# A two-bit search, a turned gate and smaller first pieces in the prologue of an expert-choice FFN

## The chip, the cores and the metric

The kernel runs on one core of a Trainium2 chip. The time is the device time of one execution in microseconds (us): the median of three runs is 4277.47 us (4274.08 to 4278.06). One more execution was profiled; the lines of the profile that this text shows come from it. In them PE is the tensor engine, PEld its weight loads, DVE the vector engine, ACT the scalar engine, POOL the GpSimd engine and SP the engine that issues most DMAs.

## The reference, cut to what matters

Six layers run over 4096 tokens of 256 features: an expert-choice FFN, an attention, the same FFN again, a routed FFN, another attention, the routed FFN again. The change touches only the expert-choice FFN, which occurs twice, on the layer-normalized rows:

```python
S = jax.nn.sigmoid(xt @ Wg).T            # 8 experts x 4096 tokens
G, I = jax.lax.top_k(S, k)               # k = 1024: each expert chooses its tokens
ex = xt[I]
hid = gelu(einsum('ekh,ehf->ekf', ex, W1) + b1)
out = (einsum('ekf,efh->ekh', hid, W2) + b2) * G[..., None]
new_x = zeros_like(xt).at[I].add(out)
x = x + 0.5 * new_x
```

## The kernel before, in words

The rows lie in SBUF as 32 tiles of 128 tokens. `_ffn0` computes one expert-choice FFN, and on PE, DVE, ACT and POOL the order of its instructions is the order of the program text. It has a prologue, which ends in the list of rows of the first expert, and then a loop over eight experts that gathers rows, multiplies and scatter-adds. `tile_kernel` calls it twice, first with `n` 0, at the start of the program, and then with `n` 1, after the first attention.

The prologue's front works in eight groups of four tiles (`QT` is 4). `ln_range` takes mean and variance of eight tiles on DVE (L151, L152), and makes `rstd` from them with one square root on ACT (L160). `rows(g)` normalizes the group's four tiles, two on DVE and two on POOL (L234), into one of three buffers `xn`, and stores them to `xn_d` in DRAM. `columns(g)` turns them on PE, in eight transposes (L244), and ACT copies the result to `xnT` (L245). `logits(g)` multiplies with the gate (L250): the 128 tokens of a tile are stationary, and the gate's 8 columns move, in two halves of the features, so that each of the group's four tiles takes two matmuls of 128x128 stationary and 8 moving columns. All logits lie in one PSUM tile `lg`. In the loop over the groups `logits` runs one group behind `columns`. `sigmoid(0, 24)` and `sigmoid(24, TT)` make the scores on DVE and ACT (L262 to L266); the first stands ahead of the last group's logits.

The search follows. The scores are turned so that each of the 128 partitions holds 256 of the scores of one expert, 16 partitions to an expert. The 1024th largest score of each expert is found bit by bit, on the scores' own bits: `search` runs over the upper 15 bits and then over the lower 15 (`M` is 15), so there are 30 rounds. In one round ACT scales the values (`v`, L315, ahead of time, in four buffers), DVE counts the values that are at least the threshold `at` (L317, with an accumulator), PE adds the counts of an expert's 16 partitions by a matmul with the 0/1 matrix `same` (L307, into `cnt`), and DVE makes the next threshold from the count (L321, L325):

```python
nc.vector.tensor_scalar(junk, v, at[:, 0:1], None, ALU.is_ge, ALU.add, accum_out=r)
total(cnt, self.same, r)
nc.vector.tensor_scalar(nxt, at, 2.0, -0.5, ALU.mult, ALU.add)
nc.vector.scalar_tensor_tensor(at, cnt, float(K0), nxt, ALU.is_ge, ALU.add)
```

In the first round `lower_bits` makes the lower half of the values on DVE behind the count. Then ties are settled, each chosen token gets its place in its expert's list (L344 to L380), and `indices` (L388 to L410) writes the list with one-hot matmuls. POOL gathers the rows by it (L419). PE's first matmul of the experts is L448.

Of the kernel before, what the change touches and what calls it, by code (L numbers as in the profile page):

```python
# [9 lines left out]
F32 = mybir.dt.float32  # L10
BF16 = mybir.dt.bfloat16
I32 = mybir.dt.int32
AF = mybir.ActivationFunctionType
ALU = mybir.AluOpType
# [6 lines left out]
P = 128  # L21
B, S, D = 8, 512, 256
NT = B * S
TT = NT // P
DC = D // P
QT = S // P
# [3 lines left out]
E0, FF = 8, 1024  # L30
K0 = NT * 2 // E0
# [11 lines left out]
E1, INTER, SHARED = 16, 128, 256  # L43
N_GROUPS, TOPK_GROUPS, TOPK = 4, 2, 4


FULL = TT * TOPK
SLOTS = FULL + E1

CH = 512  # L50
# [9 lines left out]
class Kernel:  # L60
    def __init__(self, ctx, tc, w):
        self.tc, self.nc, self.w = tc, tc.nc, w
        nc = self.nc
        self.const = const = ctx.enter_context(tc.tile_pool(name="const", bufs=1))
        resid = ctx.enter_context(tc.tile_pool(name="resid", bufs=1))
        self.dram = ctx.enter_context(tc.tile_pool(name="dram", bufs=1, space=DRAM))


        self.late = self.wide = None


        self.x = resid.tile([P, TT, D], F32, name="x")
        x_in = w["x"].rearrange("(t p) d -> p t d", p=P)
        for g in range(TT // QT):
            ts = slice(g * QT, g * QT + QT)
            nc.sync.dma_start(out=self.x[:, ts, :], in_=x_in[:, ts, :])

        self.ident = const.tile([P, P], F32, name="ident")
        make_identity(nc, self.ident)
        self.ones = const.tile([P, P], F32, name="ones")  # L80
        nc.gpsimd.memset(self.ones, 1.0)

        self.tri = const.tile([P, P], F32, name="tri")
        nc.gpsimd.affine_select(
            out=self.tri, in_=self.ones, compare_op=ALU.is_gt, fill=0.0,
            base=0, pattern=[[1, P]], channel_multiplier=-1,
        )

        iota_i = const.tile([P, P], I32, name="iota_i")
        nc.gpsimd.iota(iota_i, pattern=[[1, P]], base=0, channel_multiplier=0)  # L90
        self.iota = const.tile([P, P], F32, name="iota")
        nc.vector.tensor_copy(self.iota, iota_i)

        lane_i = const.tile([P, 1], I32, name="lane_i")
        nc.gpsimd.iota(lane_i, pattern=[[1, 1]], base=0, channel_multiplier=1)
        self.lanes = const.tile([P, 1], F32, name="lanes")
        nc.vector.tensor_copy(self.lanes, lane_i)
        self.bands = const.tile([P, 2, TT // 2], F32, name="bands")
        nc.vector.tensor_copy(self.bands, iota_i[:, 0:TT].rearrange("p (j c) -> p c j", c=2))

        self.iota_h = const.tile([P, P], BF16, name="iota_h")
        nc.vector.tensor_copy(self.iota_h, iota_i)

        self.same = const.tile([P, P], F32, name="same")
        runs = self.same.rearrange("p (e j) -> p e j", j=P // E0)
        ones = self.ones.rearrange("p (e j) -> p e j", j=P // E0)
        nc.gpsimd.affine_select(
            out=runs, in_=ones, compare_op=ALU.is_ge, fill=0.0,
            base=0, pattern=[[-(P // E0), E0], [0, P // E0]], channel_multiplier=1,
        )  # L110
        nc.gpsimd.affine_select(
            out=runs, in_=runs, compare_op=ALU.is_ge, fill=0.0,
            base=P // E0 - 1, pattern=[[P // E0, E0], [0, P // E0]], channel_multiplier=-1,
        )
        self.before = const.tile([P, P], F32, name="before")
        nc.gpsimd.tensor_tensor(self.before, self.same, self.tri, ALU.mult)

        self.desc = const.tile([P, E1], F32, name="desc")
        nc.vector.tensor_scalar(self.desc, self.iota[:, 0:E1], -1.0, float(E1), ALU.mult, ALU.add)

        self.slots_d = self.dram.tile([SLOTS * P, D], F32, name="slots_d")
        self.ys_d = self.dram.tile([SLOTS * P, D], F32, name="ys_d")
# [76 lines left out]
    def _ffn0(self, ctx, n, beside):  # L199
        nc, tc, w = self.nc, self.tc, self.w  # L200
        pool = ctx.enter_context(tc.tile_pool(name=f"f0_{n}", bufs=1))
        work = ctx.enter_context(tc.tile_pool(name=f"f0w_{n}", bufs=2))
        psum = ctx.enter_context(tc.tile_pool(name=f"f0p_{n}", bufs=2, space=PSUM))
# [9 lines left out]
        wg = pool.tile([P, DC, E0], F32, name="wg")  # L213
# [12 lines left out]
        lg = psum.tile([P, TT, E0], F32, name="lg", tag="rt", bufs=1)  # L226
        stats = mv, rstd = self.ln_tiles(pool)
        xns, xnTs = {}, {}

        def rows(g):  # L230
            xn = xns[g] = work.tile([P, QT, D], F32, name="xn", bufs=3)
            for i in range(QT):
                t = g * QT + i
                (nc.vector, nc.gpsimd)[i % 2].tensor_scalar(  # L234
                    xn[:, i, :], self.x[:, t, :], mv[:, t, 0:1], rstd[:, t : t + 1], ALU.subtract, ALU.mult
                )
            nc.sync.dma_start(out=xn_rows[:, g * QT : g * QT + QT, 0:D], in_=xn)

        def columns(g):
            xnT = xnTs[g] = work.tile([P, DC, CH], F32, name="xnT", bufs=2)  # L240
            for c in range(DC):
                tp = psum.tile([P, CH], F32, name="tp", tag="tp")
                for i in range(QT):
                    nc.tensor.transpose(tp[:, i * P : i * P + P], xns[g][:, i, c * P : c * P + P], self.ident)  # L244
                nc.scalar.copy(xnT[:, c, :], tp)  # L245

        def logits(g):
            for i in range(QT):
                for c in range(DC):
                    nc.tensor.matmul(  # L250
                        lg[:, g * QT + i, :], lhsT=xnTs[g][:, c, i * P : i * P + P], rhs=wg[:, c, :],
                        start=(c == 0), stop=(c == DC - 1),
                    )

        raw = pool.tile([P, TT, E0], F32, name="raw")

# [2 lines left out]
        def sigmoid(t0, t1):  # L259
            r = raw[:, t0:t1, :]  # L260

            nc.vector.tensor_scalar(r, lg[:, t0:t1, :], -87.0, None, ALU.max)  # L262
            nc.scalar.activation(r, r, AF.Exp, scale=-1.0)
            nc.vector.tensor_scalar(r, r, 1.0, None, ALU.add)
            nc.vector.reciprocal(r, r)
            nc.vector.tensor_copy(s[:, :, :, t0 // 2 : t1 // 2], r.rearrange("p (j c) e -> p c e j", c=2))  # L266

        self.ln_range(pool, stats, 0, 8)
        for g in range(TT // QT):
            if g % 2 == 0 and g < 6:  # L270
                self.ln_range(pool, stats, (g // 2 + 1) * 8, 8)
            rows(g)
            columns(g)
            if g > 0:
                logits(g - 1)
        wts = weights(0)
        sigmoid(0, 24)
        logits(TT // QT - 1)
        sigmoid(24, TT)
        nc.sync.dma_start(out=xn_rows[:, :, D:], in_=raw)  # L280
        for g in range(4):
# [8 lines left out]

        M = 15
        sp = psum.tile([P, 2, P], F32, name="sp", tag="tp")
        for c in range(2):
            nc.tensor.transpose(sp[:, c, :], s[:, c].rearrange("p e j -> p (e j)"), self.ident)
# [3 lines left out]
        high = pool.tile([P, D], F32, name="high")  # L300
        nc.vector.tensor_copy(high, high_i)
        low_i = pool.tile([P, D], I32, name="low_i")
        low = pool.tile([P, D], F32, name="low")
        junk = pool.tile([P, D], F32, name="junk")

        def total(out, weights, r):
            nc.tensor.matmul(out, lhsT=weights, rhs=r, start=True, stop=True)  # L307

        def search(vals, between):

            at = work.tile([P, 1], F32, name="at", bufs=4)
            nc.vector.memset(at, 0.5)
            for b in range(M - 1, -1, -1):
                v = work.tile([P, D], F32, name="v", bufs=4)
                nc.scalar.mul(v, vals, 0.5 ** (b + 1))  # L315
                r = work.tile([P, 1], F32, name="r", bufs=2)
                nc.vector.tensor_scalar(junk, v, at[:, 0:1], None, ALU.is_ge, ALU.add, accum_out=r)  # L317
                cnt = psum.tile([P, 1], F32, name="cnt", tag="psI", bufs=1)
                total(cnt, self.same, r)
                nxt = work.tile([P, 1], F32, name="nxt", bufs=2)  # L320
                nc.vector.tensor_scalar(nxt, at, 2.0, -0.5, ALU.mult, ALU.add)  # L321
                if b == M - 1:
                    between()
                at = work.tile([P, 1], F32, name="at", bufs=4)
                nc.vector.scalar_tensor_tensor(at, cnt, float(K0), nxt, ALU.is_ge, ALU.add)  # L325
            return at

        def lower_bits():
            nc.vector.tensor_scalar(low_i, bits, (1 << M) - 1, None, ALU.bitwise_and)
            nc.vector.tensor_copy(low, low_i)  # L330

        at = search(high, lower_bits)

        vals = pool.tile([P, D], F32, name="vals")
        nc.vector.tensor_scalar(vals, high, at[:, 0:1], 0.5, ALU.subtract, ALU.add)
        nc.vector.scalar_tensor_tensor(vals, vals, float(1 << M), low, ALU.mult, ALU.add)
        at = search(vals, lambda: None)


        one_row = pool.tile([P, D], F32, name="one_row")  # L340
# [1677 lines left out]
```

## Time and profile before

| what | us |
|---|---|
| median of three runs | 4277.47 |
| the profiled execution | 4273.81 |
| its span, first to last instruction | 4271.7 |
| PE busy | 3817.9 (89%) |
| DVE busy | 1929.9 (45%) |
| ACT busy | 1461.2 (34%) |
| POOL busy | 1229.9 (29%) |
| first prologue: first statistics, first transposes, last logits read by DVE, first count, last count's result, first gather | 4.9, 17.1, 58.5, 62.2, 107.0, 121.7 |
| second prologue: the same | 1468.9, 1482.3, 1523.8, 1527.5, 1572.0, 1586.7 |

The page's second part cuts the span into 40 slices of 106.8 us and gives the busy tenths of each engine; PEclk is the granted share of the tensor engine's clock in tenths. The granted clock over the whole span is 0.904. A busy share is an average over stages with different limits, so that what the change is worth is read from the timeline and the waits of the two prologues.

### The profile page before, as it was taken

The numbers are of one execution on the slowest core, as the hardware profiler recorded it, in microseconds if no ns is written. First come the engines' busy times: TensorE is split into PE (matmuls) and PEld (weight loads), VectorE is DVE, ScalarE is ACT, GpSimd is POOL, SyncE is SP. The second block draws the span as 40 slices with busy tenths as digits, with TensorE's granted clock in tenths as the row PEclk, the third lists the DMA queues.
The fourth block names the chain that finished last, engine by engine and source line by source line (L and its number), as shares of the span: only waits on it lengthen the run. The fifth ranks groups of instructions, "written<-read, shape, count | busy, mean of one in ns | idle before, by whom it ended". The sixth has DMA issues, their size and how long they took to land.

```text
span 4271.7 us, 51994 instructions
## 1 busy us (share of the span) xinstructions
PE 3817.9 (89%) x17660; PEld 2304.8 (54%) x17660; DVE 1929.9 (45%) x5057; ACT 1461.2 (34%) x3371; POOL 1229.9 (29%) x1132
## 2 busy tenths in 40 slices
PE   5789896999999759889878998999999999998998
PEld 5456663333333446566546784545545555457774
DVE  4321204555554441121166366665555546555455
ACT  2122222333343212222223343444444443443441
POOL 2233224223231113223136251221000011461256
PEclk6899997889996559999979999999999999998999
DMA  5223225700000212223334470100000000115664
GB/s 186 50 65 66 56 39 185 244 17 17 23 11 21 73 40 53 69 61 67 65 119 165 153 248 22 30 27 9 1 1 1 1 1 1 40 56 160 195 198 130
DMA packets 262995, 316.67 MB, mean 74 GB/s; under 512 B 31696, under 2 KB 232784, under 8 KB 262480
## 3 DMA queue, kind: packets, MB, share of 16 engines
q1 hardware_dynamic: 213584, 212.12, 15.9%
q0 software_dynamic: 49152, 101.24, 9.7%
q8 instruction: 146, 2.39, 0.2%
q14 instruction: 113, 0.93, 0.1%
HBM read 157.81 MB, written 147.06 MB: 71 GB/s over the span
## 4 chain that ended last, share of the span: by engine, by line
PE 60%; DVE 9%; ACT 5%; issue 5%; DMA 3%; POOL 0%; POOLq 0%; DVEq 0%; ACTq 0%; SPq 0%
PE pq L997 5%; PE hs L1664 5%; PE op L459 5%; PE sp L1023 5%; PE zp L1057 5%; PE hp L448 5%; PE tp L1044 4%; PE st L769 3%; PE pv L978 3%; PE yp L1087 3%; PE yps L1684 2%; PE hp L1580 2%; PE pp L637 2%; ACT ex L1032 2%; DMA yg<-ys_d,slot 2%
## 5 line engine op out<-in xcount | busy, mean ns | idle before, releaser
L1032 ACT ACTIVATE ex<-sp,nmax 128x512 f32<-128x512 f32 x512 | 347.4, 689 | 411.1 <-DVE nmax L1029 388.9
L459 PE MATMUL op<-w,hid 128*128 128x256 f32 x2048 | 473.2, 394 | 0.0
L448 PE MATMUL hp<-exT,w 128*128 128x512 f32 x1024 | 448.0, 596 | 0.0
L459 PEld LDWEIGHTS op<-w,hid 128*128 128x128 f32 x2048 | 406.8, 199 | 66.1 <-issue 8.6
L466 POOL DMA_INDIRECT acc_d<-ob,idx x128 | 199.7, 1560 | 689.1 <-ACT ob L465 387.2
L1432 POOL DMA_INDIRECT yg<-ys_d,slot x256 | 266.5, 1041 | 411.2 <-DVE x L1451 194.4
L464 DVE TENSOR_TENSOR ob<-op,b 128x256 f32<-128x256 f32 x128 | 54.4, 425 | 663.8 <-PE op L459 640.3
L1029 DVE TENSOR_REDUCE nmax<-sp 128x2 f32<-128x1024 f32 x256 | 303.2, 1218 | 72.3 <-PE sp L1023 72.1
L1044 PEld LDWEIGHTS tp<-ident,ex 128*128 128x128 f32 x2048 | 226.9, 141 | 190.6 <-issue 129.3
L1664 PE MATMUL hs<-w_sb,xT 128*128 (+1 forms) x1152 | 312.1, 395 | 19.1 <-DVE as L1672 11.3
L448 PEld LDWEIGHTS hp<-exT,w 128*128 128x128 f32 x1024 | 195.2, 192 | 232.0 <-issue 231.2
L740 DVE CUSTOM_DVE_ANT_0 junk<-sp,mask 128x128 f32<-128x128 f32 (+3 forms) x512 | 248.5, 485 | 133.0 <-PE sp L733 113.4
L1044 PE MATMUL tp<-ident,ex 128*128 128x128 f32 x2048 | 275.4, 278 | 36.2 <-ACT eT L187 35.8
L452 ACT ACTIVATE hid<-hp,b 128x512 f32<-128x512 f32 x256 | 175.9, 687 | 338.4 <-PE hp L448 338.4
L1023 PE MATMUL sp<-qk,qk 64*128 64x512 f32 x1024 | 261.7, 630 | 1.9 <-ACT ex L1032 1.9
L997 PE MATMUL pq<-xnT,wide 128*128 128x512 f32 x512 | 252.0, 616 | 5.6 <-DVE eT L189 4.7
L778 ACT ACTIVATE ex<-st 128x1024 f32<-128x1024 f32 (+3 forms) x256 | 173.9, 703 | 240.5 <-DVE st L776 240.4
L1064 POOL COPY wide<-rec 128x512 f32<-128x512 f32 x64 | 39.2, 612 | 714.8 <-PE rp L1070 605.2
L1250 POOL DMA_INDIRECT slots_d<-wide,slot x176 | 175.0, 994 | 233.4 <-DVE lane L1387 102.2
L465 ACT ACTIVATE ob<-ob,gate 128x256 f32<-128x256 f32 x128 | 65.0, 508 | 510.7 <-DVE ob L464 510.7
L1057 PE MATMUL zp<-eT,v 128*64 128x512 f32 x1024 | 235.2, 600 | 0.0
L1664 PEld LDWEIGHTS hs<-w_sb,xT 128*128 128x128 f32 x1152 | 202.9, 196 | 46.1 <-issue 10.8
(325 smaller groups left out, 6092.2 us busy)
## 6 DMA issues: line engine op xcount, KB each, us to landing
xs<-slots_d SPq DMA_DIRECT2D x70, 512.0 KB, 5.4
ys_d<-ys SPq DMA_DIRECT2D x70, 512.0 KB, 3.5
w<-in_W SPq DMA_DIRECT2D x32, 1024.0 KB, 5.6
slots_d<-mask SPq DMA_DIRECT2D x8, 2304.0 KB, 10.9
ys_d<-mask SPq DMA_DIRECT2D x8, 2304.0 KB, 17.9
w_sb<-in_w SPq DMA_DIRECT2D x24, 512.0 KB, 7.6
xn_d<-xn SPq DMA_DIRECT2D x16, 512.0 KB, 4.3
acc_d<-x SPq DMA_DIRECT2D x8, 1024.0 KB, 5.1
```

The lines of the kernel that those rows point to most:

```text
L448: nc.tensor.matmul(hp, lhsT=w1[:, c, f * P : f * P + P], rhs=exT[e][:, c, h * CH : h * CH + CH], start=(c == 0), stop=(c == DC - 1),)
L459: nc.tensor.matmul(op, lhsT=hid[h][:, f, i * P : i * P + P], rhs=w2[:, f, :], start=(f == 0), stop=(f == FC - 1),)
L466: nc.gpsimd.indirect_dma_start(out=acc_d[:, :], out_offset=bass.IndirectOffsetOnAxis(ap=idx[:, e, st : st + 1], axis=0), in_=ob, in_offset ...
L740: nc.vector.tensor_tensor_reduce(out=junk[:, :wd], in0=sps[h // 2][:, h % 2, :wd], in1=mask[:, S - wd :], scale=1.0, scalar=NEG, op0=ALU.a ...
L997: nc.tensor.matmul(pp, lhsT=(wq, wk)[a][:, k, c * P : c * P + P], rhs=seq[b]["xnT"][:, k, :], start=(k == 0), stop=(k == DC - 1),)
L1023: nc.tensor.matmul(sp[:, j, :], lhsT=q[r, qt * P : qt * P + P], rhs=k[r, :], start=True, stop=True)
L1029: latest[0] = nc.vector.tensor_reduce(nmax, sp, AX.X, ALU.max, negate=True).ins
L1032: nc.scalar.activation(ex[:, j, :], sp[:, j, :], AF.Exp, bias=nmax[:, j : j + 1], accum_out=ch["sums"][:, qt, j : j + 1],)
L1044: nc.tensor.transpose(tp[:, k, :], ch["ex", qt][:, j, k * P : k * P + P], self.ident)
L1057: nc.tensor.matmul(zp[DK1 * j : DK1 * j + DK1, :], lhsT=seq[b]["v", h][:, k, at : at + DK1], rhs=ch["eT"][:, j, k, :], start=(k == 0), sto ...
L1432: inst = nc.gpsimd.indirect_dma_start(out=self.y[t, r], out_offset=None, in_=self.k.ys_d[:, :], in_offset=bass.IndirectOffsetOnAxis(ap=sel ...
L1664: nc.tensor.matmul(hp.rearrange("p a i -> p (a i)"), lhsT=st[j]["xT"][:, c, :], rhs=self.w13[:, st[j]["e"], c, :].rearrange("p e i -> p (e ...
```

## The change

It has three parts, all in the prologue. The search finds two bits a round, with three thresholds; two of the counts are made on DVE, and the third on ACT as a sum of signs. `M` becomes 14, and the rounds are 8 on the upper 16 bits and 7 on the lower 14. The gate's 8 columns become stationary, and 512 tokens move; the logits come out as 8 rows of 512, ACT copies them to `lT`, and four transposes (`back`) bring them into `lg`. The first eight tiles are taken in two pieces of four, and `rows` runs two groups ahead of `columns`. Three small constant tiles (`reach`, `signs`, `steps`) are written at the start by 30 memsets on POOL.

```diff
         def logits(g):
+            lp = psum.tile([P, CH], F32, name="lp", tag="h")
+            for c in range(DC):
+                nc.tensor.matmul(
+                    lp[0:E0, :], lhsT=wg[:, c, :], rhs=xnTs[g][:, c, :], start=(c == 0), stop=(c == DC - 1)
+                )
+            lT[g] = work.tile([E0, CH], F32, name="lT", bufs=1)
+            nc.scalar.copy(lT[g], lp[0:E0, :])
+
+        def back(g):
             for i in range(QT):
-                for c in range(DC):
-                    nc.tensor.matmul(
-                        lg[:, g * QT + i, :], lhsT=xnTs[g][:, c, i * P : i * P + P], rhs=wg[:, c, :],
-                        start=(c == 0), stop=(c == DC - 1),
-                    )
+                nc.tensor.transpose(
+                    lg[:, g * QT + i, :], lT[g][:, i * P : i * P + P], self.ident[0:E0, 0:E0]
+                )
...
-        self.ln_range(pool, stats, 0, 8)
+        for g in range(2):
+            self.ln_range(pool, stats, g * QT, QT)
+            rows(g)
         for g in range(TT // QT):
             if g % 2 == 0 and g < 6:
-                self.ln_range(pool, stats, (g // 2 + 1) * 8, 8)
-            rows(g)
+                self.ln_range(pool, stats, (g + 2) * QT, 2 * QT)
+            if g + 2 < TT // QT:
+                rows(g + 2)
             columns(g)
+            if g > 1:
+                back(g - 2)
             if g > 0:
                 logits(g - 1)
         wts = weights(0)
         sigmoid(0, 24)
+        back(TT // QT - 2)
         logits(TT // QT - 1)
+        back(TT // QT - 1)
         sigmoid(24, TT)
...
-        M = 15
+        M = 30 - 2 * ROUNDS
...
-        def search(vals, between):
+        def search(vals, rounds, between):
...
-            at = work.tile([P, 1], F32, name="at", bufs=4)
-            nc.vector.memset(at, 0.5)
-            for b in range(M - 1, -1, -1):
+            thr = self.steps[:, rounds - 1, :]
+            at = None
+            for b in range(rounds - 1, -1, -1):
                 v = work.tile([P, D], F32, name="v", bufs=4)
-                nc.scalar.mul(v, vals, 0.5 ** (b + 1))
-                r = work.tile([P, 1], F32, name="r", bufs=2)
-                nc.vector.tensor_scalar(junk, v, at[:, 0:1], None, ALU.is_ge, ALU.add, accum_out=r)
-                cnt = psum.tile([P, 1], F32, name="cnt", tag="psI", bufs=1)
+                nc.scalar.mul(v, vals, 0.25 ** (b + 1))
+                r = work.tile([P, 3], F32, name="r", bufs=2)
+                for i in range(2):
+                    nc.vector.tensor_scalar(
+                        junk, v, thr[:, i : i + 1], None, ALU.is_ge, ALU.add, accum_out=r[:, i : i + 1]
+                    )
+                nc.scalar.activation(signs, v, AF.Sign, bias=thr[:, 2:3], accum_out=r[:, 2:3])
+                cnt = psum.tile([P, 3], F32, name="cnt", tag="psI", bufs=1)
                 total(cnt, self.same, r)
-                nxt = work.tile([P, 1], F32, name="nxt", bufs=2)
-                nc.vector.tensor_scalar(nxt, at, 2.0, -0.5, ALU.mult, ALU.add)
-                if b == M - 1:
+                if b == rounds - 1:
                     between()
+
+                here = work.tile([P, 1], F32, name="here", bufs=2)
+                base = work.tile([P, 3], F32, name="base", bufs=2)
+                if at is None:
+                    nc.vector.memset(here, 0.0)
+                    nc.vector.tensor_copy(base, self.steps[:, b - 1, :])
+                else:
+                    nc.vector.tensor_scalar(here, at, 4.0, None, ALU.mult)
+                    if b > 0:
+                        nc.vector.scalar_tensor_tensor(
+                            base, self.signs, here[:, 0:1], self.steps[:, b - 1, :], ALU.mult, ALU.add
+                        )
+                hit = work.tile([P, 3], F32, name="hit", bufs=2)
+                digit = work.tile([P, 1], F32, name="digit", bufs=2)
+                nc.vector.scalar_tensor_tensor(
+                    hit, cnt, 0.0, self.reach, ALU.add, ALU.is_ge, accum_out=digit
+                )
+                if b > 0:
+                    thr = work.tile([P, 3], F32, name="thr", bufs=2)
+                    nc.vector.scalar_tensor_tensor(thr, self.signs, digit[:, 0:1], base, ALU.mult, ALU.add)
                 at = work.tile([P, 1], F32, name="at", bufs=4)
-                nc.vector.scalar_tensor_tensor(at, cnt, float(K0), nxt, ALU.is_ge, ALU.add)
+                nc.vector.tensor_scalar(
+                    at, here, digit[:, 0:1], 0.0 if b > 0 else 0.5, ALU.add, ALU.add
+                )
             return at
...
-        at = search(high, lower_bits)
+        at = search(high, ROUNDS, lower_bits)
...
-        at = search(vals, lambda: None)
+        at = search(vals, M // 2, lambda: None)
```

More of the change, by code (lines that the diff above doesn't have):

```diff
@@ L44 @@
 N_GROUPS, TOPK_GROUPS, TOPK = 4, 2, 4
+ROUNDS = 8
 FULL = TT * TOPK
@@ L116, in __init__ @@
         nc.gpsimd.tensor_tensor(self.before, self.same, self.tri, ALU.mult)
+        self.reach = const.tile([P, 3], F32, name="reach")
+        self.signs = const.tile([P, 3], F32, name="signs")
+        self.steps = const.tile([P, ROUNDS, 3], F32, name="steps")
+        for i in range(3):
+            nc.gpsimd.memset(self.reach[:, i : i + 1], float(K0 if i < 2 else 2 * K0 - NT))
+            nc.gpsimd.memset(self.signs[:, i : i + 1], 1.0 if i < 2 else -1.0)
+            for r in range(ROUNDS):
+                at = (i + 1) / 4 - 0.5 / 4 ** (r + 1)
+                nc.gpsimd.memset(self.steps[:, r, i : i + 1], at if i < 2 else -at)
         self.desc = const.tile([P, E1], F32, name="desc")
@@ L245, in columns @@
                 nc.scalar.copy(xnT[:, c, :], tp)
+        lT = {}
         def logits(g):
-            for i in range(QT):
-                for c in range(DC):
-                    nc.tensor.matmul(
-                        lg[:, g * QT + i, :], lhsT=xnTs[g][:, c, i * P : i * P + P], rhs=wg[:, c, :],
-                        start=(c == 0), stop=(c == DC - 1),
-                    )
+            lp = psum.tile([P, CH], F32, name="lp", tag="h")
[6 more added lines that the diff above has]
+        def back(g):
+            for i in range(QT):
+                nc.tensor.transpose(
+                    lg[:, g * QT + i, :], lT[g][:, i * P : i * P + P], self.ident[0:E0, 0:E0]
+                )
         raw = pool.tile([P, TT, E0], F32, name="raw")
@@ L304, in _ffn0 @@
         junk = pool.tile([P, D], F32, name="junk")
+        signs = pool.tile([P, D], F32, name="signs")
         def total(out, weights, r):
             nc.tensor.matmul(out, lhsT=weights, rhs=r, start=True, stop=True)
-        def search(vals, between):
-            at = work.tile([P, 1], F32, name="at", bufs=4)
-            nc.vector.memset(at, 0.5)
-            for b in range(M - 1, -1, -1):
+        def search(vals, rounds, between):
+            thr = self.steps[:, rounds - 1, :]
+            at = None
+            for b in range(rounds - 1, -1, -1):
```

## The prediction

> **What bounds the kernel now.** I read the busy slices of the page first. Each expert-choice FFN opens with a prologue, about 0 to 136 us and 1469 to 1600 us in the timeline; in those slices (the first, and the 14th and 15th) PE falls to 5 and 7 tenths, and the granted clock to 5 or 6.
>
> ```profile
> PE   5789896999999759889878998999999999998998
> ...
> PEclk6899997889996559999979999999999999998999
> ```
>
> The waits of the first 130 us name the chain. POOL cannot gather before the indices exist, and those hang on a search in which DVE and PE release each other.
>
> ```profile
> POOL ex L419 <- DVE idx L410: 80.6, 1, 80.6
> PEld cnt L307 <- DVE junk L317: 30.4, 29, 2.2
> DVE at L325 <- PE cnt L307: 17.8, 29, 0.6
> ```
>
> So a prologue is serial: what shortens its chain shortens the kernel. Two parts of the chain are edited. The first is the front, from the first statistics to the last logits. The windows of the first and second prologue's front, then of the search, show who is full (columns: stretch, length, busy time of PE, weight load, DVE, ACT, POOL, clock, DMA share, GB/s):
>
> ```profile
> 29.00:54.00 25.00, 25.00 (x121) 25.00 (x122) 4.69 (x16) 7.24 (x12) 6.51 (x6) 0.50 0.62 203
> 1495.00:1520.00 25.00, 24.70 (x119) 24.60 (x117) 4.39 (x14) 7.24 (x12) 6.04 (x6) 0.50 0.34 115
> 64.00:107.00 43.00, 17.00 (x58) 14.53 (x58) 20.90 (x118) 11.25 (x26) 0.00 (x0) 0.50 0.41 138
> ```
>
> In the front PE is 100% busy at half clock; in the search nobody is. One group of four tiles, and one round, from the timeline:
>
> ```profile
> 40.75 3.54 PEld L250 LDWEIGHTS lg<-wg,xnT 128*128 128x128 f32 x16
> 44.03 1.76 PEld L244 LDWEIGHTS tp<-ident,xn 128*128 128x128 f32 x8
> ...
> 63.65 0.48 DVE L317 TENSOR_SCALAR_CACHE_REDUCE junk<-v,at 128x256 f32<-128x256 f32 x1
> 64.06 0.08 DVE L317 DVE_READ_ACCUMULATOR junk<-v,at 128x1 f32 x1
> 64.19 0.58 PE L307 MATMUL cnt<-r,same 128*128 128x1 f32 x2 [0.86 <-DVE junk L317]
> 64.82 0.16 DVE L325 SCALAR_TENSOR_TENSOR at<-cnt,nxt 128x1 f32<-128x1 f32 x1 [0.61 <-PE cnt L307]
> 65.10 0.48 DVE L317 TENSOR_SCALAR_CACHE_REDUCE junk<-v,at 128x256 f32<-128x256 f32 x1
> ```
>
> Groups follow each other every 5.01 us (39.01, 44.03, 49.04): 24 weight loads of 0.209. A round is 65.10 - 63.65 = 1.45 us; 30 rounds are 43.5 us.
>
> **What the skill says.** "TensorE: Matmul & The Clock Gate", Part 1, gives half clock unless the array was busy through a window of about 3.4 us. The trace's clock does change in steps of 3.41 us. Its Part 4 says that transposes don't count as busy. The trace disagrees: after the window 17.05 to 20.46, which holds transposes alone (first line: the tile `tp` only; the clock's record starts at 20.5), the 16 gate loads at 20.40 took 1.91 us instead of 3.54. What stays cold is a busy PE whose matmuls use few rows or columns: from 1344 to 1361 us, attention with 16 or 17 rows or 32 columns, mixed with some full ones, PE never idle:
>
> ```profile
> 17.05:20.46 3.41, 3.38 (x16) 3.01 (x16) 0.00 (x0) 1.63 (x3) 1.00 0.82 281
> 1347.82:1351.24 3.42, 3.42 (x17) 0.50 0.00 0
> 1351.24:1354.65 3.41, 3.41 (x15) 0.50 0.00 0
> ```
>
> The same page, section "LDWEIGHTS (loading the stationary operand)": a load costs by its columns, not its rows. The trace before has no load of 8 rows; I use the page's rule, so 0.209 us again. "ScalarE: Activation LUTs", section "What ACT_TABLE_LOAD costs": an ACTIVATE with a pointer bias takes 0.28 us plus 0.833 ns per element, by which I estimate 0.49 us for Sign on 256; before's 256-wide ACTIVATE without one shows 0.42.
>
> **The search, part by part.** 15 rounds in place of 30 (8 on the upper 16 bits, 7 on the lower 14), each longer. From the first count's start: its accumulator is read after 0.41 and is done at 0.49; the second count writes the same `junk` and starts at about 0.55; its read starts at 0.96. PE starts 0.13 later, as before (64.06 to 64.19), and takes 0.58; three columns for one cost no more in a matmul that is all load and latency. DVE goes on 0.05 later. `hit` is a tiny operation with an accumulator read: 0.25 until `thr`, one dependent step of 0.20 (the spacing in the layer norm's chain) plus 0.05. `thr` to the next count 0.28, as `at` to count now. Sum 0.96 + 0.13 + 0.58 + 0.05 + 0.25 + 0.28 = 2.25 us, 33.8 per prologue.
>
> Beside it: Sign can start some 0.24 after `thr`; with 0.49 and an accumulator read of 0.20 (ACTIVATION_READ_ACCUMULATOR, 204 ns) it ends 0.93 after `thr`, while the second count's read ends 0.28 + 1.04 = 1.32 after it: hidden with 0.39 to spare, and if it were not, every us over that would be paid 15 times. `v` of the next round follows on ACT (0.42) under PE's matmul. `here` and `base` (two steps, 0.40) lie under PE's 0.58. In the first round `low_i` and `low` (0.41 and 0.29) with two more small ones overrun PE by about 0.2. No table load is added: in the built order ACT loads for Exp and next for GELU, as before. Saving per prologue 43.5 - 33.8 - 0.2 = 9.5. For the unmeasured steps I keep 2.05 (no gap between the counts, `thr` after 0.2) to 2.50 (0.05 for each of five semaphores more) as ends: 12.6 to 5.8.
>
> **The front.** The gate's old matmuls are 16 loads, 3.34 us of the 5.01. The new ones stream 512 tokens: two matmuls of two passes. A 128x512 pass at half clock is 0.85 us (loads at 137.25, 138.10, 138.95), so 3.41: nothing won. Four transposes back (`back`) are added: 4 x 0.209, of which the first load hides under a transpose; 0.63. The eight transposes stay, 1.67. Group: 1.67 + 0.63 + 3.41 and 0.05 for a hand-over = 5.76, so +0.75.
>
> Rows by fours start PE earlier: 4 tiles of statistics (0.53 each), the chain to `rstd` (1.6, with the table load of 1.28 in prologue 2), then POOL's two rows (1.21 each). In prologue 2, counted from 1468.9, `xn` of group 0 is whole at 1476.7 and of group 1 at 1481.2, where PE now starts at 1482.3. But group 2 hangs on eight tiles of statistics queued behind on DVE and on POOL: whole at 1487.5. PE then does what is left of its transposes (1.1), `back(0)` (0.85) and `logits(1)` (3.41) until 1492.9. Five more groups at 5.76: 1521.7. Then a tail that is new: `logits(7)` is queued on PE behind `back(6)`, which waits for `lT(6)` on ACT (0.65 with its hand-over), then `back(6)` 1.0, `logits(7)` 3.5, `lT(7)` 0.65, `back(7)` 1.1: 1528.6, where DVE takes the last logits at 1523.8 now. +4.8. Prologue 1 alike: group 1's logits end at 27.9, the tail at 63.6 against 58.5: +5.1. ACT's load for Exp and Exp itself lie under `logits(7)`; if they didn't, 1.6. The eight `xn_d` stores (0.5 MB each) are issued two groups earlier and on SP stand ahead of `w1` and `w2`; the weights are first used at 136, some 70 us after, so I take nothing, and each `xn` buffer comes free a group before it is refilled; a late store would cost what DVE waits for now, 3.0 at 38.3. Thirty memsets on POOL (0.10 each, 3.0 at most) lie in its idle time from 3.3 us to the first `rstd` at about 9; without that cover, 3.0 once. Outside the two prologues the order is the same.
>
> **Sum.** -9.5 - 9.5 + 4.8 + 5.1 = -9.1 us. The profiled execution took 4273.81 (span 4271.7), 3.7 under the median 4277.47; so 4264.7 on its own scale and 4268.4 on the median's: 4268. 0.2% is 8.6 us, about what a measurement of this kernel can tell from no change; the forecast lies on that line.
>
> **Rivals.**
> - *The clock rises in the front.* If streaming through 8 columns counts as a busy array, PE is warm: a group takes about 3 us and POOL's rows set the pace, the last at about 39.0 and 1504.2; logits end near 1511, 12.8 earlier than now. Both prologues: -25.6 - 19.0 = -44.6, 4233. For it: 3.41 of 5.76 us stream without a pause. Against it: the cold stretch above.
> - *The front costs less.* `back`'s loads hide or the tail overlaps: +3 for both, 4261.
> - *A round is too long.* Place: `hit`, its accumulator read, `thr` and ACT's hand-over of `r[:, 2]` to PE. It decides from 2.57 us on, where the front's 9.9 eats the 30 x (2.90 - 2.57) saved. At 2.9 nothing is won: 4287. For it: each hand-over is counted from operations like it, none measured. Against it: 0.3 us more is over a tenth in a round whose largest terms are measured.
>
> **Numbers.** The forecast has 0.62, with its own range 4258 to 4278, half of it past 0.2%; the clock 0.12; the cheaper front 0.10; the long round 0.16, a quarter of it within 0.2%. Faster 0.31 + 0.12 + 0.08 = 0.51, same 0.36, slower 0.13. The range reaches from 4252, which leaves out most of the clock's case, to 4284.
>
> **What would show it.** Right: rounds of 2.2 to 2.3 us with PE released by DVE; clock 0.50 in the front; PE without a gap from group 2 on, at about 5.8 us each; last logits 5 us later. Wrong: a clock of 1.00 before the search; PE released by ACT; groups nearer 5.0 us; a table load inside the search.

## The result, and the profile after

The changed kernel takes 4211.99 us (median of four runs, 4208.42 to 4238.65) against 4277.77 of the kernel before: a ratio of 0.9857, with a 95% interval of 0.9821 to 0.9893. That is 65.8 us, where the prediction had 9, and outside its range (4252 to 4284). Its profiled execution took 4210.26, with a span of 4208.6. Cut at the same instructions, the two spans differ so:

| stage | before | after | difference |
|---|---|---|---|
| start to first expert matmul (`hp`) | 136.4 | 117.1 | -19.3 |
| experts of the first FFN | 533.6 | 532.5 | -1.1 |
| attention (first `pp` to the next statistics) | 798.9 | 780.9 | -18.0 |
| second prologue, to `hp` | 132.4 | 112.8 | -19.6 |
| experts of the second FFN | 522.1 | 521.4 | -0.7 |
| all that follows | 2148.3 | 2143.9 | -4.4 |

So 38.9 of the 63.1 us lie where the change was made, and most of the rest lies in a stage whose code it left alone. Of each prologue's part about half is the front (the last logits at 48.4 instead of 58.5 us; the second front 44.5 us long instead of 54.9), half the search and what hangs on it (from the last logits to `hp` 68.7 and 68.3 us instead of 77.8 and 77.5).

The busy slices of the page show the first: PEclk in the first slice, and in the 14th and 15th, goes from 6, 5, 5 to 7, 6, 6, while PE's own busy tenths there hardly change (5, 7, 5 to 4, 7, 5).

```profile
PE   4889897999999758999768999999999999998988
...
PEclk7899997889898669999879999999999999998999
```

The waits of the first 130 us. POOL still hangs on the indices, and in the search PE is now released by `here`, DVE's first step behind the second count; its weight load is put down to `v` on ACT, which came earlier.

```profile
POOL ex L477 <- DVE idx L468: 61.8, 1, 61.8
...
PEld cnt L340 <- ACT v L349: 25.8, 13, 3.0
PE cnt L340 <- DVE here L367: 21.3, 12, 2.1
```

The windows of the two fronts and of the search (columns as before: stretch, length, busy time of PE, weight load, DVE, ACT, POOL, clock, DMA share, GB/s). In the fronts PE is as full as before, but at full clock, and its weight loads fill less than half of the time:

```profile
24.19:40.82 16.63, 16.00 (x82) 7.24 (x81) 10.88 (x43) 8.13 (x17) 11.30 (x10) 1.00 0.82 273
1450.00:1466.00 16.00, 15.42 (x79) 7.06 (x78) 11.67 (x46) 8.05 (x17) 10.99 (x10) 0.99 0.86 274
54.00:87.00 33.00, 7.52 (x28) 6.80 (x28) 24.46 (x137) 13.28 (x42) 0.00 (x0) 0.50 0.45 152
```

From the timeline of the second front, PE alone. A group is 1454.08 to 1457.25, so 3.17 us instead of 5.01. The first line shows a wait that the prediction missed.

```profile
1446.13 1.97 PE L259 MATMUL tp<-ident,xn 128*128 128x128 f32 x8 [6.21 <-ACT xnT L260]
...
1454.08 1.09 PE L259 MATMUL tp<-ident,xn 128*128 128x128 f32 x8
1455.10 0.41 PE L276 MATMUL lg<-ident,lT 8*128 8x8 f32 x4
1455.44 1.88 PE L268 MATMUL lp<-xnT,wg 128*8 128x512 f32 x4
1457.25 1.09 PE L259 MATMUL tp<-ident,xn 128*128 128x128 f32 x8
```

And one round of the search. From count to count it is 58.67 - 56.37 = 2.30 us; ACT's Sign and the read of its accumulator end at 56.97, under the second count, whose own read begins at 57.30:

```profile
56.36 0.51 ACT L355 ACTIVATE signs<-v,thr 128x256 f32<-128x256 f32 x1 [1.42 <-DVE at L381]
56.37 0.48 DVE L352 TENSOR_SCALAR_CACHE_REDUCE junk<-v,thr 128x256 f32<-128x256 f32 x1
...
56.78 0.19 ACT L355 ACTIVATION_READ_ACCUMULATOR signs<-v,thr 128x1 f32 x1
...
57.30 0.08 DVE L352 DVE_READ_ACCUMULATOR junk<-v,thr 128x1 f32 x1
...
57.53 0.56 PE L340 MATMUL cnt<-r,same 128*128 128x3 f32 x2 [1.74 <-DVE here L367]
58.12 0.16 DVE L374 SCALAR_TENSOR_TENSOR hit<-cnt,reach 128x3 f32<-128x3 f32 x1 [0.41 <-PE cnt L340]
...
58.32 0.22 DVE L379 SCALAR_TENSOR_TENSOR thr<-signs,digit,base 128x3 f32<-128x3 f32 x1
...
58.67 0.48 DVE L352 TENSOR_SCALAR_CACHE_REDUCE junk<-v,thr 128x256 f32<-128x256 f32 x1
```

### The profile page after: what moved, and what is told of

Read it like the earlier page. It is cut to its first block, busy times and chain, and to the rows that moved or that the text cites. A ratio compares the mean times of both kernels' runs of the same rounds, so it can differ in the third digit from the quotient of the medians.

```text
span 4208.6 us, 51725 instructions
## 1 busy us (share of the span) xinstructions
PE 3748.9 (89%) x17472; PEld 2222.3 (53%) x17472; DVE 1942.5 (46%) x5117; ACT 1473.6 (35%) x3419; POOL 1230.8 (29%) x1162
## 4 chain that ended last, share of the span: by engine, by line
PE 60%; DVE 9%; ACT 5%; issue 5%; DMA 3%; POOL 1%; POOLq 0%; DVEq 0%; ACTq 0%; SPq 0%
PE pq L1055 5%; PE op L517 5%; PE hp L506 5%; PE hs L1722 5%; PE zp L1115 5%; PE sp L1081 5%; PE tp L1102 4%; PE st L827 3%; PE yp L1145 3%; PE pv L1036 3%; PE yps L1742 2%; PE pp L695 2%; ACT ex L1090 2%; PE hp L1638 2%; DMA yg<-ys_d,slot 2%
## 5 line engine op out<-in xcount | busy, mean ns | idle before, releaser
L517 PEld LDWEIGHTS op<-w,hid 128*128 128x128 f32 x2048 | 405.6, 199 | 66.7 <-issue 8.6
L1722 PE MATMUL hs<-w_sb,xT 128*128 (+1 forms) x1152 | 309.6, 392 | 18.6 <-DVE as L1730 10.2
```

What stands on the lines that cost most here:

```text
L517: nc.tensor.matmul(op, lhsT=hid[h][:, f, i * P : i * P + P], rhs=w2[:, f, :], start=(f == 0), stop=(f == FC - 1),)
L1722: nc.tensor.matmul(hp.rearrange("p a i -> p (a i)"), lhsT=st[j]["xT"][:, c, :], rhs=self.w13[:, st[j]["e"], c, :].rearrange("p e i -> p (e ...
```

## The experiments

### Which part warms the front

Four kernels shared one chip: each part of the change alone on the kernel before, and the changed kernel with fewer rows in the gate's product. On that chip the layers behind the second expert-choice FFN took 2323 to 2343 us in all four profiles instead of the 2143 to 2156 of every other profile here, and the kernel before 4458 us; so their totals are compared as ratios, and the prologues by their own times.

**The gate alone.**

```diff
-   nc.tensor.matmul(lg[:, g * QT + i, :], lhsT=xnTs[g][:, c, i * P : i * P + P], rhs=wg[:, c, :], ...)
+   nc.tensor.matmul(lp[0:E0, :], lhsT=wg[:, c, :], rhs=xnTs[g][:, c, :], ...)   # lT, back(g) as in the change
```

> The kernel before with one part of the change: the gate's weights stationary, 512 tokens streaming past 8 columns, and the transposes back. Theory (a long stream through 8 columns counts as a busy array): clock 1.00 through the front from about 20 us on, a group every 3.0 to 3.5 us, the last logits of the first prologue at 47 to 50 us against 58.5 before, the same 10 us in the second prologue: about 4257 to 4260 in all if attention keeps its time of before. Rival (the earlier start by fours made the clock rise, not the gate's form): clock 0.50, groups of 5.8 us, last logits at 60 to 63 us, total 4280 to 4285.

Ratio 0.997 (0.9957 to 0.9984). Timeline of PE:

```profile
24.89 1.11 PE L244 MATMUL tp<-ident,xn 128*128 128x128 f32 x8 [2.23 <-DVE xn L234]
...
26.26 1.88 PE L253 MATMUL lp<-xnT,wg 128*8 128x512 f32 x4
28.07 1.09 PE L244 MATMUL tp<-ident,xn 128*128 128x128 f32 x8
...
33.65 1.11 PE L244 MATMUL tp<-ident,xn 128*128 128x128 f32 x8 [2.33 <-DVE xn L234]
```

The clock rises, and a group takes 28.07 - 24.89 = 3.18 us. But the last logits come at 52.3 us, not at 47 to 50: twice PE waits over 2.2 us for normalized rows. Three windows of this kernel, each one step of the clock, show what such a wait does (same columns). In the first PE is busy for 1.09 of 3.42 us, and the next one is granted half clock; that one is busy throughout, and the third is at full clock again. The first wait of the two cost nothing: in its window, 20.97 to 24.38, PE was busy for 1.68 us, and the clock stayed at 1.00.

```profile
31.20:34.62 3.42, 1.09 (x9) 0.84 (x8) 2.35 (x10) 0.95 (x3) 1.22 (x1) 1.00 1.05 346
34.62:38.04 3.42, 3.42 (x10) 0.88 (x8) 1.35 (x4) 0.81 (x2) 1.81 (x3) 0.50 1.03 338
38.04:41.46 3.42, 3.42 (x17) 1.46 (x16) 0.42 (x1) 1.61 (x3) 2.40 (x3) 1.00 0.69 226
```

**The fours alone.**

```diff
-   self.ln_range(pool, stats, 0, 8)
+   for g in range(2):
+       self.ln_range(pool, stats, g * QT, QT)
+       rows(g)
...
-   rows(g)
+   if g + 2 < TT // QT:
+       rows(g + 2)
```

> The kernel before with the first rows by fours and rows issued two groups ahead, gate and search as before. Theory (the gate's form makes the clock): clock 0.50 in most of the front, groups of 5.0 us, last logits within 3 us of 58.5: total within 6 us of before. Rival (the earlier start does it): clock 1.00, groups of about 3.2, last logits near 48 us in the first prologue, total about 4257.

Ratio 1.0003 (0.9989 to 1.0018); last logits at 59.0 us, second front 55.0 us. Nothing won. Its timeline shows why PE gains nothing from the early rows, and that the groups stay at 5.01 us:

```profile
19.59 1.97 PE L244 MATMUL tp<-ident,xn 128*128 128x128 f32 x8 [6.60 <-ACT xnT L245]
21.34 3.42 PE L250 MATMUL lg<-wg,xnT 128*128 128x8 f32 x16
24.62 1.95 PE L244 MATMUL tp<-ident,xn 128*128 128x128 f32 x8
...
29.63 1.95 PE L244 MATMUL tp<-ident,xn 128*128 128x128 f32 x8
```

In the program text, which ACT follows, the square root of tiles 8 to 15 stands ahead of the first group's copies to `xnT`. PE has the first group transposed by 13.0 us and then waits 6.60 us, until eight tiles of statistics have been made on DVE: the square root starts at 18.85, the copies at 18.96.

**Both together**, with the old search (on a chip where the kernel before takes 4278 us).

> The gate turned and the first rows by fours together, with the search of before. The gate alone took 6.2 us and 3.4 us off the two fronts, the fours alone added 0.5 and 0.1, the whole change took off 10.2 and 10.4. Theory (once the clock is full, the supply of rows is the bound, and only then do rows issued two groups ahead help): last logits at 48.4 and fronts of 44.5 us as in the changed kernel, search of 44.5. Rival (the two-bit search or its set-up has a share in the front): last logits at 50 to 52.

Ratio 0.9937 (0.9914 to 0.996). Last logits at 48.3 us, second front 44.5: the changed kernel's numbers, so the search has no share in the front. A gain of 6.2 us (gate) and a loss of 0.4 (fours) alone make a gain of 10.2 together: at full clock PE waited for rows, and only then do the rows issued two groups ahead count.

**The search alone.**

```diff
-   nc.vector.tensor_scalar(junk, v, at[:, 0:1], None, ALU.is_ge, ALU.add, accum_out=r)
+   for i in range(2):
+       nc.vector.tensor_scalar(junk, v, thr[:, i : i + 1], None, ALU.is_ge, ALU.add, accum_out=r[:, i : i + 1])
+   nc.scalar.activation(signs, v, AF.Sign, bias=thr[:, 2:3], accum_out=r[:, 2:3])
...
-   at = search(high, lower_bits)            # 15 rounds, and 15 on the lower bits
+   at = search(high, ROUNDS, lower_bits)    # 8 rounds, and 7 on the lower bits
```

> The kernel before with the search by two bits a round, all else as before. Both theories on the front: front unchanged (58.5 us), 15 rounds of 2.30 us in place of 30 of 1.45, so 9.5 us less in each prologue, total 4258. What it tells apart is attention, which took 798.9 us before and 780.9 in the changed kernel with its code unchanged: if that belongs to the changed front, attention takes 799 here and the total is 4258; if it hangs on when the stage begins, it can take anything from 780 to 799 here.

Ratio 0.9962 (0.9944 to 0.9981), so 17 us of 4458. From the first count to the search's last `at` it is 35.4 us in place of 44.5 in the second prologue, and the first front ends as before, at 58.6. Attention took 801.6 us from the first `pp`, 798.9 in the kernel before: its gain is not the search's.

**Fewer rows.**

```diff
-   lp[0:E0, :], lhsT=wg[:, c, :], rhs=xnTs[g][:, c, :], ...
+   lp[0:E0, :], lhsT=wg[0:16, c, :], rhs=xnTs[g][0:16, c, :], ...
```

> The changed kernel, with the gate's two matmuls of a group contracting only rows 0 to 15 of each half (16 of 128 features of each half; the other 112 are left out), which move the same 512 tokens in the same time. Theory (the array counts as busy by the rows that it uses, and columns do not matter): clock 0.50 in the front, groups of 5 to 6 us, last logits of the first prologue at 58 to 66 us against 48.4. Rival (only the time counts in which something moves through the array): as the changed kernel, clock 1.00 and last logits at 48.4.

This kernel leaves out 112 of the 128 features of each half. Ratio 0.9995 (0.9982 to 1.0009), with the new search in it: the front's whole gain is gone, and more. The record of the clock begins with its first change, which in this kernel comes only at 137 us, so the durations have to tell: the transposes take 1.97 us in place of 1.09, the streams 3.58 in place of 1.88.

```profile
24.92 1.97 PE L259 MATMUL tp<-ident,xn 128*128 128x128 f32 x8
26.82 0.59 PE L276 MATMUL lg<-ident,lT 8*128 8x8 f32 x4
27.34 3.58 PE L268 MATMUL lp<-xnT,wg 16*8 16x512 f32 x4
30.85 1.97 PE L259 MATMUL tp<-ident,xn 128*128 128x128 f32 x8
```

A group is 5.93 us (the prediction's cold group: 5.76), and the last logits come at 66.7, a little past the range expected. The same instructions, the same moving time: with 16 rows in place of 128 the front stays at half clock. The 8 columns are the same in both kernels, so few columns alone do not keep a clock low. Rows alone do not keep it full either: the old gate's matmuls contract 128 rows, but move only 8 columns behind each load, and that front is at 0.50. In this profile attention took 780.8 us, as in the changed kernel, though the front is slower than in the kernel before; so a faster front is not what shortens it.

### Attention's 18 us

In attention the two score products contract 16 and 17 rows for each of four heads. By the run above that may be what lets the clock fall; the last pair of runs tests it. First, how firm the 18 us are. Two more profiles, of unchanged kernels:

> The kernel before, unchanged, for a second profile. Attention, from its first score matmul to the next FFN's first statistics, took 739.2 us in the first profile of before, and 739.1, 735.4 and 742.1 in the kernels with a part of the change; 721.4 in the changed kernel and in the one with 16 rows. Theory (its length is set by where in the 3.41 us steps of the clock it begins, which the change does not decide): any of these lengths can come up; beginning at 0.78 to 0.81 of a step gives 735 to 742, at 0.89 gives 721.4. Rival (the change itself shortens attention): 739.2 again, whatever the start.

> The changed kernel, unchanged, for a second profile and many times. Theory (attention's length hangs on where in a step of the clock it begins): 721.4 us if it begins at 0.89 of a step, 735 to 742 if at 0.78 to 0.81, and the times of the runs fall into groups up to 28 us apart. Rival (the change itself shortens attention): 721 us whatever the start, the times in one group. Front, search and clock as in the first profile under both: last logits at 48.4, rounds of 2.30.

The kernel before gave 4273.56 us and 739.1 of attention, the changed one a median of 4218.53, a ratio of 0.9864 (0.9837 to 0.9891), and 725.0. Attention is counted here from the first matmul of its second score product, `st` (the expectations say first score matmul), to the next statistics; the stage table starts some 60 us earlier, at the first `pp`. These two decide nothing: 739.1 again is what the rival had, and the changed kernel's four runs lay within 7.3 us, where groups up to 28 us apart were expected.

Set against the steps of the clock, the first two profiles of the kernel before and that of the fours, on two chips, begin attention at 0.79 of a step, and all 41 stretches of full and half clock through it have the same length. The changed kernel and the one with 16 rows both begin at 0.89, and again have the same stretches, of another kind. So attention can repeat itself stretch by stretch, in different kernels. But its start within a step does not settle its length: 735 to 742 us were expected for 0.78 to 0.81, and five more profiles that begin at 0.79 or 0.80, those with a delay and the version with a shorter tail below among them, have 728.5 to 742.1; the changed kernel's second profile begins at 0.85. What parts the ways is not shown. One kernel's own runs differ too: with gate and fours together the profiled run, with 752.3 us of attention, took 4269.14 us, the other four 4249.65 to 4252.95.

A delay tests whether the shorter way belongs to the change:

```diff
+   for _ in range(4 if n == 0 else 0):      # 2 in the other run
+       nc.vector.tensor_scalar(junk, high, 1.0, None, ALU.mult)
    at = search(high, ...)
```

> The kernel before with two idle operations of DVE (0.40 us each) ahead of the first prologue's search: a delay of 0.8 us and nothing else. Theory (attention's length hangs on fine timing, and each kernel draws its own): the total changes by something other than 0.8, by up to 20 us either way, and attention (739.1 in all three profiles of before's timing) may take 720 to 752. Rival (attention's gain belongs to the change): attention stays at 739 and the total at 0.8 us more than before.

> As the run with two idle operations, with four: a delay of 1.6 us, half a step of the clock. Theory: a total that differs from before by more than 3 us either way, or attention away from 739. Rival: attention 739, total 1.6 us more than before.

> The changed kernel with the same delay of 0.8 us in its first prologue. Two profiles of the changed kernel gave 721.4 and 725.0 us of attention. Theory (each kernel draws its own): a median away from the changed kernel's 4212 to 4219 by 5 to 25 us, attention anywhere from 720 to 752. Rival (the gain belongs to the change): attention 721 to 729, median 1 us more than the changed kernel.

> The changed kernel with a delay of 1.6 us. Theory and rival as for 0.8 us: away from 4212 to 4219 by 5 to 25 us, or 1.6 us more with attention of 721 to 729.

| kernel | median us | ratio, interval | attention, first `st` to next statistics |
|---|---|---|---|
| before, 2 idle operations | 4280.07 | 1.0007 (0.9993 to 1.002) | 742.1 |
| before, 4 | 4270.84 | 0.9984 (0.9976 to 0.9991) | 728.5 |
| after, 2 | 4223.48 | 0.9873 (0.9853 to 0.9894) | 732.0 |
| after, 4 | 4223.88 | 0.9868 (0.985 to 0.9887) | 735.3 |

The first search's end, counted from the last logits, moved by 0.6 us at most, less than the 0.8 and 1.6 meant, since DVE waits there for ACT's first `v` in any case (0.48 us at 62.20 in the kernel before). With two idle operations the kernel before moved by 1.1 us, much as the rival had it, and its attention by 3. Yet with four it is 8 us *faster* than without, on the same chip, and its attention is as short as a changed kernel's; the changed kernel with them, on another chip than in its repeat, stands 5 to 12 us above its own two medians, though the intervals of the ratios overlap, and its attention is 7 to 14 us longer than in its own two profiles. One line each of the windows, over the whole stage (same columns), of the kernel before, then of it with four idle operations, then of the changed kernel with four: DVE, ACT and POOL do the same work, and PE's busy time goes with the clock.

```profile
670.00:1468.90 798.90, 727.55 (x4029) 308.44 (x4028) 407.26 (x1486) 289.53 (x485) 215.00 (x184) 0.82 0.20 63
```

```profile
671.10:1459.20 788.10, 715.95 (x4029) 305.00 (x4028) 407.14 (x1486) 289.55 (x485) 215.04 (x184) 0.84 0.21 64
```

```profile
650.10:1444.70 794.60, 722.19 (x4029) 307.50 (x4028) 407.88 (x1487) 289.66 (x485) 215.09 (x184) 0.83 0.20 63
```

That does not show that the change has no share: its kernels had 721 to 735, those without all of it 728 to 752. The last pair of runs takes the few rows away:

```diff
-   r = slice(32 * h, 32 * h + HD0)          # top(): 16 rows of each head
+   r = slice(32 * h, 32 * h + 32)
-   r = slice(32 * h, 32 * h + HD0 + 1)      # exps(): 17 rows
+   r = slice(32 * h, 32 * h + 32)
```

The added rows lie in the tiles already, are zero on one side of each product, and add nothing to it.

> The kernel before with attention's two score products contracting 32 rows of each head in place of 16 and 17; the added rows are zero on one side, the moving time is the same, and the four heads then fill all 128 rows. Attention took 739.2 us with 280 at half clock in the kernel before, 721.4 with 235 in the changed one. Theory (few rows in use let the clock fall, and when it falls hangs on fine timing): attention's clock at 1.00 nearly throughout; 739.2 - 280 / 2 and 721.4 - 235 / 2 both give about 600 if PE stays the bound, 600 to 650 with other engines taking over, total 4140 to 4190. Rival (four heads at once count as they did, or the zeros count as nothing): attention of 720 to 752 and a clock that falls as before.

> The changed kernel with the same two slices of 32 rows. Theory: attention as long as in the kernel before with that edit, to within 3 us, since nothing is left to fall; so the two totals differ by fronts and searches alone, 10.2 + 9.5 + 10.4 + 9.7, about 39 to 40 us in place of 66: total 4100 to 4150. Rival (the change shortens attention itself): attention is again 10 to 20 us shorter than in the kernel before with that edit, or, where the edit does nothing, 721 to 735.

The kernel before then takes 4207.64 us (ratio 0.9838, 0.9815 to 0.9862), the changed one **4157.46** (0.9715, 0.9692 to 0.9739): the fastest version here. Of attention 78 and 67 us are left at half clock, of 280 and 235. The stage in both, before and changed:

```profile
669.10:1398.90 729.80, 646.84 (x4029) 278.23 (x4028) 405.48 (x1487) 288.64 (x485) 214.93 (x184) 0.95 0.22 69
```

```profile
649.80:1375.50 725.70, 642.32 (x4030) 276.10 (x4028) 405.54 (x1486) 288.43 (x485) 215.00 (x184) 0.95 0.22 69
```

So it is the rows: neither the moving time nor the columns have changed. Nor is it the number of cells of the array in use, since the new gate, 128 rows by 8 columns, keeps the clock with fewer cells than the 16 rows by 128 columns of one head have. The theory was right in kind and too hopeful in size: 672 and 667 us from the first `st` on, not 600 to 650, and both totals lie above the ranges expected. (Its sum took the 280 and 235 us from the first `pp` on; from `st` on they are 251 and 206, which gives 614 and 618.)

PE's busy time fell by 81 and 66 us, but 12 and 11 us of it came back as idle time of PE, now 83 us in both (stage less busy time), since it waits more for the other engines. The stages differ by 4.1 us in place of 18.0, not by at most 3 as expected. The profiled spans differ by 40.8, near the forecast 39 to 40; the medians differ by 50.2. The profiled run was the fastest of six in the one kernel and the slowest in the other, so the agreement of the spans with the forecast is in part luck. Most of the 18 us, then, goes with the clock's falls in attention, which come out otherwise from kernel to kernel; whether the change makes the shorter way likelier is not shown, and some 10 us of the difference in medians are not explained by any run.

### A version with a shorter tail

```diff
-   (nc.vector, nc.gpsimd)[i % 2].tensor_scalar(
+   (nc.gpsimd if i == 1 or i == 3 and g < 6 else nc.vector).tensor_scalar(
...
-   back(TT // QT - 2)
    logits(TT // QT - 1)        # its logits go to the tile of high and low, not to lT
+   back(TT // QT - 2)
    back(TT // QT - 1)
...
-   at = here + digit           # behind thr
+   at = here + digit           # behind the next round's counts, ahead of its here
```

> The changed kernel with three edits in the prologue's serial parts: the last eight tiles' rows go 6 to DVE and 2 to POOL in place of 4 and 4; the last group's logits no longer wait for the transposes back of the one before (own buffer for its logits, sigmoid of the first 24 tiles issued a group earlier); and the search issues `at` behind the next round's counts. By the trace of the changed kernel: POOL's rows end 2.5 us earlier, the tail after the last transposes is 1.3 us shorter, a round 2.15 in place of 2.30 us. So last logits of the first prologue at 44.6 against 48.4, search 2.2 us shorter, 6 us for each prologue, 12 in all if attention begins at the same place in a step of the clock. Rival (PE sets the pace of the last groups): the first edit gives nothing, last logits at 47.1.

Median 4225.08, ratio 0.9881 (0.9855 to 0.9908): no better than the changed kernel's 0.9857 and 0.9864. The last logits come at 46.9 (48.4) and the second front is 43.0 long (44.5), so the tail's edit gives 1.5 us, 1.3 expected, and the rival was right on the first edit: PE begins the last transposes at 40.81 against 40.82, since PE sets the pace of the last groups.

```profile
40.81 1.09 PE L259 MATMUL tp<-ident,xn 128*128 128x128 f32 x8
...
42.17 3.60 PE L269 MATMUL lp<-xnT,wg 128*8 128x512 f32 x8
...
46.44 0.41 PE L280 MATMUL lg<-ident,pair 8*128 8x8 f32 x4 [0.33 <-ACT pair L276]
```

Moving `at` behind the counts gives nothing: a round stays at 2.30 us, because the next count begins 0.35 us after `thr` starts with or without `at` between them. The 3 us of the two prologues are less than what the clock's falls in attention move the total by.

## Why the prediction was wrong, point by point

- **The clock of the front: the step that failed.** "Nothing won" by the gate rested on a clock of 0.50, and that on attention's cold stretch, read as "few rows or columns". Attention mixes both, so it could not tell them apart. The new gate's 128 rows count, for all its 8 columns: the clock was 1.00, the four passes of a group took 1.81 us, not 3.41, and a group 3.17, not 5.76. So the fronts became 10.2 and 10.4 us shorter, where 5.1 and 4.8 us more were forecast. The rival that had it, at 0.12, said -12.8. This step is 30.5 of the 54.0 us by which the profile missed the forecast; with the fronts as measured the forecast would have been about 4238 (an estimate from these figures), outside its own range already.
- **The rows by fours.** Forecast: an earlier start with a tail that costs more. Alone they gave +0.4 and +0.1 us. The wait of PE for ACT's square root, 6.60 us, was missed: what a moved step finds queued ahead of it on its engine was asked for DVE, POOL and SP, but not for ACT's square root. With a full clock the fours bring another 4 to 7 us.
- **The tail** is there as described, `back(6)` waiting for `lT(6)` 0.72 us, but at full clock: 7.5 us from the last transposes to the last logits. `back` takes 0.34 us of a group (0.52 at half clock, in the run with 16 rows), forecast 0.63; its loads of 8 rows take 0.14 us each, as long as those of the transposes beside them with 128, so that rows did not matter there, as assumed.
- **The search** was right, with errors of both signs in its terms. A round is 2.30 us against 2.25 (PE starts 0.23 after the second count's read begins, not 0.13, and the step from `thr` to the count is 0.35, not 0.28; `thr` itself comes 0.20 after `hit`, not 0.25). Sign is hidden, as forecast. Last logits to `hp` fell by 9.1 and 9.2 us; forecast 9.5.
- **Sum.** Fronts and searches give 38.9 us. The rest, 24.2 in the profile, was outside of every case: each put at nothing what happens outside the two prologues, since "the order is the same" there. The order was, the times were not: attention alone, from `st` on, has 721 to 752 us in the fourteen profiles without added rows, 739 in the kernel before. The three runs shown ahead of it lay within 4 us and did not tell this; 35 runs of the kernel before beside the later experiments spread from 4260.6 to 4289.9.

## What to carry to other kernels

When a stage runs at half clock, look at how many rows its matmuls contract, and how many columns move behind each load: turning a product so that a long stream passes a full height of rows, or filling unused rows with zeros that lie there anyway, can be worth more than the removal of work. A full clock moves the bound: after it, feed PE earlier, and look for a queued operation of another batch ahead of what PE waits for. And where a stage sits on the edge of the clock, a difference of some us in it says nothing of the change: compare stages, with several profiles, before explaining a total.

## What was not expected of the hardware

- The granted clock goes with rows, not with columns, where the moving time is the same: 128 rows with 8 columns keep it full, 16 rows with 8 columns do not; and attention with 32 rows a head in place of 16 and 17, all else alike, has 78 us at half clock in place of 280.
- It can be lost in one step and regained in the next: 1.09 us of busy PE in a window of 3.42 cost half clock in the window that followed, and no more; 1.68 us in another window of the same front cost nothing.
- Two kernels on different chips went through 41 identical stretches of full and half clock, and a delay of 0.6 us left one kernel 8 us faster.
